# Keys and values of two groups from seven block products, logits in a ring of twelve slots, attend split around the logits

## The chip, the core and the metric

The kernel runs on one core of a Trainium2 chip. The core has five engines that run side by side and wait for each other by semaphores: TensorE (PE in the profile; PEld is its weight load), VectorE (DVE), ScalarE (ACT), GpSimd (POOL) and SyncE (SP), which here only issues DMAs. TensorE writes its results into PSUM, 8 banks of 128 x 512 float32. Everything else lies in SBUF. POOL works on SBUF alone in this kernel.

The metric is the device time of one execution in microseconds, as the median of several runs.

## What is computed

Four cross-attention layers are applied in turn to `x` (4 batches x 512 queries x 256 channels), each against the same context (4 x 1024 tokens x 512 channels). Layers 0, 2 and 3 are "masked": 16 heads of 64, with a bias on a few key columns and an output bias.

```python
def masked_layer(hidden_states, encoder_hidden_states, mask_A, mask_B, Wq, Wk, Wv, Wo, bo, ...):
    q = hidden_states @ Wq;  k = encoder_hidden_states @ Wk;  v = encoder_hidden_states @ Wv
    logits = einsum("bhqd,bhkd->bhqk", heads(q), heads(k)) * 64 ** -0.5 + col_bias
    out = einsum("bhqk,bhkd->bhqd", softmax(logits), heads(v))
    return merge(out) @ Wo + bo + hidden_states
```

Layer 1 is "grouped": an RMS norm of x, 16 query heads of 16 that share 4 key and value heads, no bias, and again the residual.

All matrices are float32. The change touches how `k` and `v` are made, in which order the pieces of attention run, and where their intermediate results lie.

## The kernel before

**Units and steps.** A masked layer of one batch is cut into 8 groups of two heads (128 rows of keys or values), so that 3 layers x 4 batches give 96 masked groups. Layer 1 of one batch is also cut into 8 units, 32 in all. Two lists written by hand, `MASKED_TURNS` and `GROUPED_TURNS` (lines 55 to 62), say for each of 104 steps from which of two streams of batches the next masked group and the next grouped unit come. So 72 steps have a masked group alone, 24 have a masked group and a grouped unit, and 8 have a grouped unit alone. Every instruction is issued in the order of the program; nothing is scheduled afterwards. The order on each engine is therefore what the step loop (from line 963) writes.

**One masked step.** For its group g the step computes the logits, transposed, as 8 tiles of 128 keys x (2 heads x 512 queries): `scores` (line 642). Each tile takes a pair of PSUM banks. ScalarE copies it to SBUF (L662). VectorE takes the running maximum in the first tile's PSUM pair, `mx_place` (L666). `max_quarters` reduces this over the keys (L712, L720, L737), and `max_everywhere` spreads it over all partitions in another PSUM pair, `mb` (L744). VectorE subtracts it from each tile (L749), ScalarE takes the exponentials (L755) and POOL adds the tiles up (L794).

Beside this the step attends for the group of the step before, g1, that is, it multiplies its exponentials with its values (`attend`, L684). It divides by the sums (`normalise`, lines 802 to 830), multiplies finished groups with the output weights (`project_out`, L840), and makes the queries of the next group (L548), the keys of the group after next (L472) and the values of the next group (L514). Keys and values of a group are each one plain product over 512 channels, in four accumulating matmuls of 128 channels. ScalarE copies them out of PSUM (L477, L526).

**Order within a step.** The logits of g come first, then the eight blocks of attend for g1. In a step with a grouped unit `lam`, these alternate with the grouped logits and their exponentials (L616, L639). Then comes a list, `fill`, of projections and products; the list `events`, ordered by rough times, interleaves the subtractions and exponentials of g with it. For a grouped unit that comes next, the maxima of its logits are found by a pass of their own (`maxima_pair`, L616 and L608), also woven into `fill`.

**Space.** The exponentials lie in `st_all`: two rings of 8 tiles and one more for the sum, so that a group has 8 slots of its own and the next group 8 others. A grouped unit uses the slots of the ring that is free. The transposed context of a batch, `ctx`, is one tile [128, 4, 1024], and three such tiles are held. PSUM banks are handed out in program order by the class `Place` (line 95). A width of 2 takes the pair of banks that was given back longest ago, a width of 1 the bank that was given back longest ago, with some preference for one whose neighbour is taken.

**Transfers.** `load_masked` and `load_grouped` issue the weights' DMAs on SP: 256 KB for the keys of one group, 256 KB for its values, 128 KB each for its query and output weights.

## Time and profile before

| What | Value |
|---|---|
| Median of 3 runs | 3808.88 us (3807.39 to 3809.19) |
| Time of the profiled execution | 3809.19 us |
| Its span, first to last instruction | 3807.4 us |
| Granted TensorE clock, mean | 0.997 of full speed |
| Keys: L472, busy on TensorE | 689.6 us in 1,536 instructions |
| Values (masked and grouped): L514 | 742.3 us in 6,400 instructions |
| Logits: L652 | 708.3 us in 3,072 instructions |
| Attend: L684 | 805.7 us in 4,064 instructions |
| DMA, mean over the span | 26 GB/s |

A float32 matmul shows as two MATMUL instructions, so that 1,536 rows of L472 are 768 matmuls of the program. The "busy" time of a group counts overlapping instructions once. The "mean" of one MATMUL is longer than its share of the busy time, because one starts before the last has ended. The idle time in a row is that of the engine just before those instructions, with the one that ended it.

### The profile page before, as it was taken

Reading aid. Unit: us, or ns where it says so; the run is one execution under the profiler, and the core shown is the slowest. Engines: PE = TensorE matmul, PEld = TensorE weight load, DVE = VectorE, ACT = ScalarE, POOL = GpSimd, SP = SyncE. Lnnn points to the kernel's source line nnn. Section 1 sums busy time; section 2 is a strip of 40 time slices with the busy share of each in tenths; the row PEclk is TensorE's granted clock in tenths of the full one; section 3 lists DMA queues with packets and bytes.
Section 4 is the critical chain, followed back from the end, with each engine's and each line's share of the span. In section 5 each row is a group of like instructions: output and inputs, shape, how many; then the busy total and the mean of one; then the engine's idle time right before and its main releaser. Section 6 shows DMA issues by size and latency. Waiting matters only on the chain.

```text
span 3807.4 us, 50450 instructions
## 1 busy us (share of the span) xinstructions
PE 3741.1 (98%) x19662; PEld 1879.9 (49%) x19662; DVE 3001.7 (79%) x3928; ACT 2101.8 (55%) x2433; POOL 1624.5 (43%) x749
## 2 busy tenths in 40 slices
PE   8999999999999999999999999999999999999998
PEld 4555444554434555555545444555444355555554
DVE  6887778778877888888887887788787778888887
ACT  4555455555545555555555555555555455555554
POOL 3555113443313555555553333445332155555554
PEclk9999999999999999999999999999999999999999
DMA  2111000010000001101011010100100000000100
GB/s 67 42 31 26 12 24 18 17 33 22 19 11 23 26 26 42 37 26 31 26 25 36 27 27 18 29 26 19 28 20 23 11 25 26 25 26 26 31 24 7
DMA packets 187874, 98.71 MB, mean 26 GB/s; under 512 B 43240, under 2 KB 183528, under 8 KB 187636
## 3 DMA queue, kind: packets, MB, share of 16 engines
q1 hardware_dynamic: 182510, 82.90, 7.9%
q0 software_dynamic: 2560, 8.39, 0.8%
q10 hardware_dynamic: 2566, 4.20, 0.5%
q8 instruction: 155, 2.54, 0.3%
q14 instruction: 83, 0.68, 0.1%
HBM read 89.16 MB, written 2.10 MB: 24 GB/s over the span
## 4 chain that ended last, share of the span: by engine, by line
PE 87%; DVE 8%; ACT 2%; issue 2%; DMA 0%; POOL 0%; DVEq 0%; ACTq 0%; POOLq 0%
PE ps L514 19%; PE ps L684 19%; PE ps L472 17%; PE ps L652 13%; PE ps L616 7%; PE ps L840 5%; PE ps L548 5%; DVE ps L666 4%; ACT st L662 1%; DVE st L749 1%; DVE st L608 1%; PE ps L490 1%; PE ps L658 1%; DVE qt L634 1%; PE ps L704 0%
## 5 line engine op out<-in xcount | busy, mean ns | idle before, releaser
L794 POOL TENSOR_TENSOR st<-st 128x1024 f32<-128x1024 f32 x668 | 1579.7, 2365 | 2059.7 <-ACT st L755 2015.7
L666 DVE TENSOR_TENSOR ps<-ps,st 128x1024 f32<-128x1024 f32 x672 | 828.2, 1232 | 466.3 <-ACT st L662 407.4
L755 ACT ACTIVATE st<-st 128x1024 f32<-128x1024 f32 x768 | 783.2, 1054 | 707.1 <-DVE st L749 695.2
L749 DVE TENSOR_TENSOR st<-st,ps 128x1024 f32<-128x1024 f32 x768 | 885.0, 1212 | 3.3
L684 PE MATMUL ps<-st,v 128*64 128x512 f32 (+1 forms) x4064 | 805.7, 597 | 0.5 <-DVE st L608 0.5
L662 ACT COPY st<-ps 128x1024 f32<-128x1024 f32 x768 | 715.4, 1047 | 101.8 <-PE ps L658 81.4
L514 PEld LDWEIGHTS ps<-wv,ctx 128*128 128x128 f32 x6400 | 729.8, 192 | 73.9 <-issue 63.6
L514 PE MATMUL ps<-wv,ctx 128*128 128x128 f32 x6400 | 742.3, 276 | 0.6 <-ACT st L662 0.6
L652 PE MATMUL ps<-qt,kt 64*128 64x512 f32 x3072 | 708.3, 598 | 1.4 <-ACT qt L554 1.4
L472 PE MATMUL ps<-ctx,wk 128*128 128x512 f32 x1536 | 689.6, 598 | 2.2 <-ACT ctx L384 2.2
L684 PEld LDWEIGHTS ps<-st,v 128*64 128x64 f32 (+1 forms) x4064 | 233.5, 130 | 545.6 <-issue 480.7
L472 PEld LDWEIGHTS ps<-ctx,wk 128*128 128x128 f32 x1536 | 288.1, 191 | 389.1 <-issue 373.2
L652 PEld LDWEIGHTS ps<-qt,kt 64*128 64x128 f32 x3072 | 283.8, 186 | 326.4 <-ACT st L662 146.0
L526 ACT COPY v<-ps 128x512 f32<-128x512 f32 x200 | 117.1, 585 | 497.1 <-PE ps L514 493.2
L608 DVE TENSOR_TENSOR st<-st,ps 128x1024 f32<-128x1024 f32 x224 | 273.3, 1220 | 129.8 <-PE ps L616 61.2
L616 PE MATMUL ps<-qt,kt 32*128 32x512 f32 x2048 | 323.8, 645 | 28.1 <-DVE qt L634 16.3
L639 ACT ACTIVATE st<-ps 128x1024 f32<-128x1024 f32 x256 | 248.4, 1023 | 185.2 <-PE ps L616 156.7
L840 PE MATMUL ps<-ot,wo 128*128 128x512 f32 x448 | 217.4, 611 | 1.4 <-DVE ot L829 0.7
L616 PEld LDWEIGHTS ps<-qt,kt 32*128 32x128 f32 x2048 | 103.4, 186 | 214.1 <-issue 57.1
L548 PE MATMUL ps<-x,wq 128*128 128x512 f32 x384 | 185.6, 606 | 1.8 <-ACT x L356 1.1
L477 ACT COPY kt<-ps 128x512 f32<-128x512 f32 x192 | 109.8, 572 | 77.3 <-PE ps L472 77.0
L840 PEld LDWEIGHTS ps<-ot,wo 128*128 128x128 f32 x448 | 78.5, 189 | 135.2 <-issue 124.2
(143 smaller groups left out, 1633.2 us busy)
## 6 DMA issues: line engine op xcount, KB each, us to landing
wk<-in_L_xattn_Wk_dram SPq DMA_DIRECT2D x96, 256.0 KB
wv<-in_L_xattn_Wv_dram SPq DMA_DIRECT2D x96, 256.0 KB
wq<-in_L_xattn_Wq_dram SPq DMA_DIRECT2D x96, 128.0 KB
wo<-in_L_xattn_Wo_dram SPq DMA_DIRECT2D x96, 128.0 KB
qt<-qt ACTq DMA_DIRECT2D x32, 128.0 KB
xraw<-in_x_dram SPq DMA_DIRECT2D x3, 512.0 KB
out_dram<-out SPq DMA_DIRECT2D x3, 512.0 KB
wq<-in_L_xattn_wq_dram SPq DMA_DIRECT2D x32, 32.0 KB
```

The source lines that it names most:

```text
L472: nc.tensor.matmul(m, lhsT=g.wk[:, k, :], rhs=ctx_t[g.b][:, k, n * 512 : (n + 1) * 512], start=(k == 0), stop=(k == KT - 1),)
L514: nc.tensor.matmul(m[:, t * P : (t + 1) * P], lhsT=ctx_t[g.b][:, k, (4 * n + t) * P : (4 * n + t + 1) * P], rhs=g.wv[:, k, :], start=(k == ...
L548: nc.tensor.matmul(m, lhsT=g.wq[:, k, :], rhs=x[:, k, :], start=(k == 0), stop=(k == KC - 1))
L616: nc.tensor.matmul(ws[odd].ap[:, j * S : (j + 1) * S], lhsT=g.kt[rows, i * P : (i + 1) * P], rhs=g.qt[rows, :], start=True, stop=True,)
L652: nc.tensor.matmul(m[:, j * S : (j + 1) * S], lhsT=g.kt[g.rows[j], keys], rhs=g.qt[g.rows[j], :], start=True, stop=t > 0,)
L662: nc.scalar.copy(g.st[t], m)
L666: nc.vector.tensor_tensor(top, top, g.st[t], ALU.max)
L684: nc.tensor.matmul(g.po[at, :], lhsT=g.v[:, t, rows], rhs=g.st[t][:, j * S : (j + 1) * S], start=(t == first), stop=(t == last),)
L749: nc.vector.tensor_tensor(g.st[t], g.st[t], g.mb, ALU.subtract)
L755: nc.scalar.activation(st, st, AF.Exp)
L794: nc.gpsimd.tensor_tensor(g.acc, g.st[0] if t == 1 else g.acc, g.st[t], ALU.add)
L840: nc.tensor.matmul(m[:, k * S : (k + 1) * S], lhsT=g.wo[:, k * P : (k + 1) * P], rhs=g.ot, start=True, stop=True,)
```

## The change

The whole change is made of these parts.

- **Seven products for eight.** The weights of two neighbouring groups form a 2 x 2 arrangement of blocks (two halves of the 512 channels by two groups), and so does the context (two halves of the channels by two halves of the tokens). A scheme of Strassen's kind in Winograd's form makes the four result blocks from seven block products and a number of sums. `pair_products` computes keys or values of a pair of groups so. In odd-numbered groups' steps the keys of the next pair are made, in even-numbered groups' steps the values of the pair itself.
- **Sums on POOL.** The sums of weight blocks (`combine_weights`, four of 128 x 256 for each pair and kind), of products (seven of 128 x 512 for each pair and kind) and of context blocks (four of 128 x 1024 for each batch) are `tensor_tensor` on GpSimd. ScalarE copies each product out of PSUM first.
- **Contexts.** A batch's context becomes a tile [128, 14, 512] that holds four blocks and three sums of blocks; two such tiles are held instead of three. One block, S3, is stored with A11 taken away, so that the grouped layer, which needs the block itself, adds A11's product again: its keys and values take more matmuls.
- **Ring.** `st_all` becomes 15 slots: a ring of 12 for exponentials, two for sums, one for the grouped maximum. The logits of group n use slots 8n to 8n + 7 modulo 12, so that its last four tiles lie where the first four of the group before were. A grouped unit uses four slots in turn.
- **Attend split.** Blocks 0 to 3 of attend for g1 come before the logits of g, blocks 4 to 7 after them. The grouped attend is spread between the grouped exponentials. Query and output projections move to the front of `fill`, or, in steps with a grouped unit, between its exponentials.
- **Maximum and sums.** The reduction over keys goes through PSUM with one more copy, the spread maximum lies in the first tile's own pair (`mx_place`) until the last subtraction, and the subtractions and exponentials have new times. The running sums from the third tile on are issued at the start of the next step. `normalise` of a group comes one step later, as VectorE's first work in a step.
- **Weights.** One DMA of 512 KB brings the weights of a pair.
- **Turns.** 106 steps: 74 with a masked group alone, 22 with both, 10 with a grouped unit alone.

The instructions that change in number, as the two programs are built (matmuls of the program, not MATMUL rows):

| Engine | Instruction | Before | After |
|---|---|---|---|
| PE | masked keys, 512 columns | 768 | 674 |
| PE | values, 128 columns (masked and grouped) | 3200 | 2848 |
| PE | grouped keys | 64 of 512 columns | 160 of 256 columns |
| POOL | sums of 128 x 1024 | 668 | 682 |
| POOL | sums of 128 x 512 | 0 | 665 |
| POOL | sums of 128 x 256 | 0 | 380 |
| ACT | copies of 128 x 512 out of PSUM, keys and values | 392 | 677 |
| DVE | small copies and sums of the reductions over keys | 1291 | 1561 |

The core of the diff:

```diff
     class Place:
-        def __init__(self, width=2):
+        def __init__(self, width=2, beside=None):
...
                 at = min(free, key=lambda n: free[n] + (2 if n ^ 1 in free else 0))
+                if beside and beside.banks[0] ^ 1 in free:
+                    at = beside.banks[0] ^ 1
...
-    st_all = t_([P, 2, NT + 1, 2 * S], "st", "st")
+    st_all = t_([P, 15, 2 * S], "st", "st")
+    ACC, TOP = 12, 14
...
+    def ring(n):
+        return st_slot(n % 12)
...
+    def combine_context(b):
+        x = lambda i: of_context(b, i)
+        on_pool(x(S1), x(S3), x(A22), ALU.add)
+        on_pool(x(S2), x(S1), x(A11), ALU.subtract)
+        on_pool(x(S4), x(A12), x(S2), ALU.subtract)
...
+    def combine_weights(kind, q):
+        w = weights[kind, q]
+        t = t_([P, 3, 2, P], "t2", f"t{kind}_{masked[2 * q].name}")
...
+        on_pool(t3, b12, b22, ALU.subtract)
+        on_pool(b12, b12, b11, ALU.subtract)
+        on_pool(t2, b22, b12, ALU.subtract)
+        on_pool(t4, b21, t2, ALU.subtract)
...
+    def pair_products(kind, q):
...
+        def product(i, w, out_, then):
+
+            place = Place(1)
+            m = place.ap
+            x = of_context(b, i)
+            if kind == "k":
+                for k in range(2):
+                    nc.tensor.matmul(m, lhsT=w[:, k, :], rhs=x[:, k, :], start=k == 0, stop=k == 1)
...
+            def done():
+                nc.scalar.copy(out_, m)
+                place.back()
+                then()
...
+        def p2():
+            return product(A12, b21, to(0, 0), lambda: add(to(0, 0), u2))
...
+        return [(1.75, p) for p in (p1, p2, p6, p7, p4, p5, p3)]
...
     def scores(g, within):
-        g.st = [st_slot((NT + 1) * g.ring + t) for t in range(NT)]
-        g.mx = st_slot((NT + 1) * g.ring + NT)
+        g.st = [ring(NT * g.n + t) for t in range(NT)]
+        g.mx = st_slot(ACC + g.n % 2)
...
+    def over_keys(of, op):
+
+
+        w = Place(1)
+        quarter, half = w.ap[:, 0:32], w.ap[0:64, 32:64]
+        other = t_([64, 32], "other", f"other{len(turns)}")
+        turns.append(0)
+        over_quarter(quarter, of, op)
+        nc.vector.tensor_copy(other, quarter[64:128, :])
+        nc.vector.tensor_tensor(half, quarter[0:64, :], other, op)
+        nc.vector.tensor_copy(other[0:32, :], half[32:64, :])
+        return half[0:32, :], other[0:32, :], w
...
+    def max_everywhere(g):
+
+        one, other, w = over_keys(g.mx_place.ap, ALU.max)
+        every = t_([P, 2 * S // 32, 1], "every", f"every_{g.name}")
         for h in range(4):
...
+            nc.vector.tensor_tensor(every[32 * h : 32 * (h + 1), :, 0], one, other, ALU.max)
+        w.back()
+        g.mb = g.mx_place.ap
...
+        for w in summed[:4]:
+            w()
+        if kind:
+            combine_weights(kind, q)
+        for w in summed[4:]:
+            w()
+        summed.clear()
+        if attended_last:
+            normalise(attended_last)
+            outs = [attended_last] + outs
+        attended_last = g1
...
+        if g1 and (g or lam):
+            place_out(g1)
         if g:
...
+            if g1:
+                attend(g1, range(0, 4))
             scores(g, lambda: lower_queries(lam) if lam else None)
...
+            max_everywhere(g)
         if lam:
...
+            if g:
+                for t in range(4):
+                    subtract(g, t)
             for i in range(NT // 2):
                 if g1:
-                    attend(g1, range(2 * i, 2 * i + 2))
+                    blocks = range(4, 8) if g else range(NT)
+                    attend(g1, blocks[2 * i : 2 * i + 2])
                 if coming and not g:
                     pair(i)
                 exponentials_pair(lam, i)
...
+                if i:
+                    if fill and (i > 1 or g):
+                        run([fill.pop(0)])
+                    if i == 1:
+                        place_out(lam, 1, g1.place if g1 else None)
+                    attend(lam, range(2 * i - 2, 2 * i))
...
         elif g1 and g:
-            attend(g1)
...
+            attend(g1, range(4, 8))
...
+        if kind:
+            made = pair_products(kind, q)
+            if len(fill) > 1 and not lam and not coming:
+
+                made[-1:-1] = [fill.pop()]
+            fill += made
```

## The prediction

> **What bounds the kernel now.** I read the page first: busy shares, then the chain, then the costliest groups.
>
> ```profile
> PE 3741.1 (98%) x19662; PEld 1879.9 (49%) x19662; DVE 3001.7 (79%) x3928; ACT 2101.8 (55%) x2433; POOL 1624.5 (43%) x749
> ...
> L794 POOL TENSOR_TENSOR st<-st 128x1024 f32<-128x1024 f32 x668 | 1579.7, 2365 | 2059.7 <-ACT st L755 2015.7
> L666 DVE TENSOR_TENSOR ps<-ps,st 128x1024 f32<-128x1024 f32 x672 | 828.2, 1232 | 466.3 <-ACT st L662 407.4
> ...
> L514 PE MATMUL ps<-wv,ctx 128*128 128x128 f32 x6400 | 742.3, 276 | 0.6 <-ACT st L662 0.6
> ...
> L472 PE MATMUL ps<-ctx,wk 128*128 128x512 f32 x1536 | 689.6, 598 | 2.2 <-ACT ctx L384 2.2
> ```
>
> TensorE carries 87% of the chain; keys (L472) and values (L514) are 1,432 us of it, and the change attacks these. The starts of the mask matmuls (L658) in the timeline give the length of each step: 31.94 us for a plain masked step (32.82 with a piece of context transposed), about 49 us (mean 47.8) where a grouped unit runs beside it, some 24 us for a grouped unit alone. A plain step in the timeline, from 1508.84 to 1541.66 (columns: start, length, engine, instruction, count):
>
> ```profile
> 1508.84 1.13 PE L652 MATMUL ps<-qt,kt 64*128 64x512 f32 x4
> ...
> 1509.81 0.38 PE L658 MATMUL ps<-aug_q,aug_k 64*128 64x512 bf16 x2
> ...
> 1510.28 7.43 ACT L662 COPY st<-ps 128x1024 f32<-128x1024 f32 x8 [0.75 <-PE ps L658]
> ...
> 1512.24 9.26 DVE L666 TENSOR_TENSOR ps<-ps,st 128x1024 f32<-128x1024 f32 x7 [5.00 <-ACT st L662]
> ...
> 1516.12 7.09 PE L684 MATMUL ps<-st,v 128*64 128x512 f32 x32
> ...
> 1521.53 1.25 DVE L712 TRANSPOSE_TENSOR_REDUCE quarter<-ps 128x32 f32<-128x1024 f32 x1
> ...
> 1523.04 0.83 DVE L737 TENSOR_TENSOR every<-half 32x32 f32<-32x32 f32 x4
> 1523.14 1.99 PE L840 MATMUL ps<-ot,wo 128*128 128x512 f32 x4
> ...
> 1526.68 7.03 PE L472 MATMUL ps<-ctx,wk 128*128 128x512 f32 x16
> ```
>
> See that TensorE has no gap: logits 7.28 us (1508.84 to 1516.12), attend 7.02, output 1.82, queries 1.72, keys 6.9, values 7.2 make the step. VectorE's maximum runs from 3.40 to 12.66 us after the first logit matmul, and its `every` (L737) ends 15.0 us after it, all hidden: the keys' and values' matmuls have other PSUM banks to go to. A matmul instruction of 512 columns starts every 0.43 us (weight loads of L472), one of 128 columns every 0.113 (7.22 us for 64).
>
> **Products.** Per pair of groups, 14 instead of 16 double matmuls of 512 columns for keys, the same share for values. Each step now makes keys or values of one pair: 28 x 0.43 = 12.04 us, or 112 x 0.113 = 12.65, where it made 6.9 + 7.2 = 14.1. That is 1.75 us a step; over 94 and 96 pairs' halves about 165 us, if TensorE stays the bound.
>
> **POOL.** Added per step: 4 weight sums of 128x256 and 7 sums of 128x512. No such row exists; L794's 1024 elements take 2.43 us from start to start, and POOL's memsets scale with elements (0.53 at 512, 0.31 at 256), so I take 1.25 and 0.67. Lower end: exactly half and a quarter; upper end: 2.43 each, as if length did not matter. POOL's step is then 7 x 2.43 + 7 x 1.25 + 4 x 0.67 = 28.4 us, inside a step of 32 to 33, though in order. Weight sums stand behind four running sums: they begin about 13 us into the step; the 512 KB they wait for are issued at its start, and the timeline's 1 us windows show 512 KB issued from 1533.7 on moved by 1537.2. Hidden. The running sums of t=2 and 3, which now must precede the copies of logits 6 and 7 into the same ring slots, end about 8 us into the step, those copies start after 10. Hidden by 2 us. SP issues fewer transfers (one of 512 KB for two of 256); the queue has nothing late.
>
> The skill speaks against loading POOL: "SBUF — State Buffer", section "Who interferes with whom", says a VectorE instruction with two SBUF inputs shuts out, or waits for, a GpSimd instruction that reads SBUF. The row first: L799 (both inputs in SBUF) takes 692 ns, L829 (one in PSUM) 691, so here no such wait shows; but POOL mostly rests at L799. The change moves the small sums of VectorE to one PSUM input; left are 24 such instructions (L799, L595). By the rule at most 24 x 2.43 = 58 us, by the row 0. I take 0: their results are not due within the step.
>
> **Logits, two PSUM pairs for three.** The changed program's bank addresses show that 91 of its 96 logits passes rotate over two pairs, where before all had three: `place_out` for the attended group now comes before the logits. Tile t+2 must wait for the copy of tile t. From the rows: first copy starts 1.44 us after the first matmul, each lasts 1.05, back to back every 0.93; a restarted tile takes 1.13 to its end, and ScalarE follows 0.09 later. Tile 3 then starts at 3.42 instead of 2.90, and two tiles take 1.13 + 0.1 + 1.05 = 2.28 instead of 1.72; the pass lasts 8.95, 1.67 more. "TensorEngine Tiling (Array Packing)", section "PSUM Bottleneck", warns that tiled matmuls outrun the copy out of PSUM. As a rate that would cost 7.43 - 7.28 = 0.15 us; the rows say it is latency and 1.67. I take the rows.
>
> **The bank behind the maximum.** In all but a handful of the steps without a grouped unit (66) the first product's bank is the one `over_keys` of the same group's maximum has just used. So it waits for `every`. After: attend of four blocks 3.59 (half of 7.02, and a switch 0.08), first copied tile 3.40, seven maxima 9.26, reduction 1.28, three small instructions 0.65 (a third one is new), `every` 0.83: 19.0 us. TensorE would be there at 3.59 + 8.95 + 3.59 + 1.82 = 17.95. It idles 1.1 us, and this hides the logits' wait. Step: 19.06 + 12.04 (or 12.65) + 1.72 = 32.8 or 33.4, mean 33.1, **+1.16 x 66 = +77 us**. Behind it on VectorE stand the output's addition and eight subtractions, to 31; `normalise` (4.2) then ends 2 us into the next step, before its maximum is due at 7. ScalarE's exponentials and copies reach 2 us into the next step, its first copy is due at 5. Both covers hold by 2 to 5 us.
>
> **Steps with a grouped unit (22).** TensorE's own work falls to about 46 (-1.8). But VectorE now does `normalise` between the last maxima of the grouped unit (the last pair closes the step) and the new maximum: 2.6 + 2.7 + 1.2 (mean) + 4.2, so the maximum begins about 10.7 instead of 7.0 us into the step. `lower_queries`' result stands behind its fifth instruction, so the first grouped exponentials wait for about 18 us, TensorE being there at 15. Then each pass needs four banks while the maximum holds two and the two `po` share a pair: query and output projections wait for a bank about 1 us each. By hand 54 to 55 us for a step of 49, +5.5; the floor is -1.8. Half the attends, which filled these waits, have gone ahead of the logits. I take +3.5, nearer the hand count: **+77 us**.
>
> **Rest.** Grouped keys: 28 us become 160 half-width matmuls; with two columns' halves beside each other 34, one after the other 69. The new order has several of the same half in a row, so +25. Grouped values 32 x 0.22 = +7. Two steps fewer shared, two more plain and two more alone: 2 x (32.1 + 23.8 - 47.8) = +16. The first step makes one pair instead of four halves, with one more key half ahead: -9.
>
> **Sum:** 77 + 77 + 25 + 7 + 16 - 9 = +193 on the profiled run's 3809.2 (span 3807.4; the median, 3808.9, is the same): **4000 us, 5% slower.**
>
> **Rivals.**
> - *VectorE's bank is no bound* (0.20): the maximum runs earlier than I have it, steps are TensorE's own sum of 32.0, grouped ones as before: 3809 + 4 + 25 + 7 + 16 - 9 = 3852.
> - *Faster* (0.13): TensorE's saving stays whole, neither bank nor pair stalls it. Speaks for it: 98% busy before and no gap. Against: the bank addresses. Plain step 30.3, -1.64 x 66 = -108; shared steps at their floor, -40; rest with grouped keys at +6, +20: 3681. It decides from the point where the first product's bank is free by 16.3 us of the step.
> - *POOL is the bound* (0.10): 512 elements cost 1.6 us, 256 cost 0.85; 31.6 us of work with waits between, steps of 34.5, about 4100.
> - The change not doing what it says is excluded: the built program has 282 + 376 + 16 key and 2,688 masked value matmuls for 768 and 3,072.
>
> **The numbers.** The main case has 0.50, its own range 3900 to 4080. Between the cases near 3809 lie 0.07. A measurement of this kernel tells 0.2%, 8 us: faster 0.13, same 0.04, slower 0.83. The range leaves out the faster side and the far end of POOL's: 3820 to 4105.
>
> **What would show it.** Plain steps of 33 between mask matmuls, the first product's matmul waiting for `every` about 1 us; weight loads of the logits waiting for copies of L662's successor 0.5 to 0.6 us at tiles 3, 5 and 7; POOL near 2,690 us busy; shared steps above 51. Plain steps at 30.3, or a first product without a wait, would make the forecast wrong.

## The result and the profile after

The changed kernel takes 4229.56 us (median of 4 runs, 4229.32 to 4229.77) against 3808.98 us before: **1.1105 times as long**, 95% interval 1.1086 to 1.1124. The forecast was 4000 us with a range to 4105: the direction was right, the size was not, 193 us forecast and 420 measured.

The page of the changed kernel (span 4227.6 us; after the bar: busy us, mean ns of one | idle before, and its releaser) has these lines for those shown of before:

```profile
PE 3868.6 (92%) x18962; PEld 1776.6 (42%) x18962; DVE 3078.5 (73%) x4198; ACT 2259.2 (53%) x2718; POOL 2761.9 (65%) x1808
...
L905 POOL TENSOR_TENSOR st<-st 128x1024 f32<-128x1024 f32 x666 | 1574.4, 2364 | 614.3 <-ACT st L871 583.9
L778 DVE TENSOR_TENSOR ps<-ps,st 128x1024 f32<-128x1024 f32 x672 | 828.2, 1232 | 495.3 <-ACT st L774 440.4
...
L764 PE MATMUL ps<-qt,kt 64*128 64x512 f32 x3072 | 844.8, 650 | 122.8 <-DVE ot L933 56.0
...
L539 PE MATMUL ps<-wv,ctx 128*128 128x128 f32 x3072 | 373.8, 278 | 29.1 <-DVE every L857 29.1
...
L534 PE MATMUL ps<-ctx,wk 128*128 128x512 f32 x752 | 361.6, 615 | 37.9 <-DVE every L857 37.8
```

Of before, the prediction shows keys and values; the logits' row is

```profile
L652 PE MATMUL ps<-qt,kt 64*128 64x512 f32 x3072 | 708.3, 598 | 1.4 <-ACT qt L554 1.4
```

TensorE fell from 98% to 92% busy, and waits now stand at three groups that had next to none. One logit matmul (L764) takes 650 ns where it took 598: part of the busy time is a slower clock or waiting inside a group. TensorE's waits, sorted (us in total, times, longest us):

```profile
PE ps L764 <- DVE ot L933: 56.0, 16, 6.0
PE ps L534 <- DVE every L857: 37.8, 33, 3.7
PE ps L764 <- ACT st L774: 37.1, 150, 0.5
PE ps L539 <- DVE every L857: 29.4, 33, 1.2
PE ps L944 <- ACT st L751: 22.1, 22, 1.3
PE ps L764 <- DVE short L918: 20.2, 5, 4.3
```

`every` is the wait the forecast named. `ot` and `short` it did not have: they belong to `normalise` of the group before.

Where the time went is read from the starts of the mask matmuls (L658 before, L770 after) in the timeline, one per masked step. The differences, grouped by kind of step (mean us, count in brackets; the last rows are sums of us), for before, after, and four of the experiments below:

| kind of step | before | after | e3_bank | h2_end_bank | h3_always | r1_out_of_loop |
|---|---|---|---|---|---|---|
| plain | 31.99 (58) | 33.61 (59) | 32.44 | 32.41 | 32.41 | 32.43 |
| shared with a grouped unit | 47.71 (22) | 56.38 (20) | 56.40 | 52.80 | 52.81 | 51.12 |
| last before a grouped run (first logits) | 47.95 (3) | 53.36 (3) | 53.05 | 53.49 | 48.46 | 47.99 |
| the one before that (grouped keys) | 42.89 (4) | 46.58 (4) | 45.41 | 45.42 | 45.41 | 45.41 |
| first behind a grouped run | 32.80 (4) | 35.88 (4) | 35.56 | 35.58 | 34.33 | 34.32 |
| a step and the units alone behind it, sum | 336.2 (3) | 510.9 (4) | 517.0 | 515.4 | 505.4 | 482.1 |
| whole span | 3807.4 | 4227.6 | 4157.8 | 4084.1 | 4053.3 | 3996.2 |

Before's very last step, 26.1 us, is among its plain ones. So the 420 us are: plain steps 59 x 1.62 = 96; shared steps 20 x 8.67 = **173**; the three kinds at the ends of grouped runs 16 + 15 + 12 = 43; stretches with units alone, like for like, 73 (a step and four units 133.5 to 159.3, a shared step and two 101.3 to 122.5 and 123.4, an opening step and two 101.6, put together from before's parts, to 105.6); the new turns at before's own prices 38 (one plain step and one stretch of 101.6 more, two shared steps fewer); first step -9; the two ends 6.

### The profile page after: what moved, and what is told of

Same layout as the page of the kernel before. It is cut to its first block, busy times and chain, and to the rows that moved or that the text cites. A ratio compares the mean times of both kernels' runs of the same rounds, so it can differ in the third digit from the quotient of the medians.

```text
span 4227.6 us, 50531 instructions
## 1 busy us (share of the span) xinstructions
PE 3868.6 (92%) x18962; PEld 1776.6 (42%) x18962; DVE 3078.5 (73%) x4198; ACT 2259.2 (53%) x2718; POOL 2761.9 (65%) x1808
## 4 chain that ended last, share of the span: by engine, by line
PE 55%; DVE 28%; ACT 11%; issue 3%; POOL 2%; DMA 0%; DVEq 0%; ACTq 0%; POOLq 0%
DVE ps L778 15%; PE ps L539 12%; PE ps L534 11%; PE ps L796 10%; PE ps L728 6%; PE ps L764 5%; PE ps L660 5%; ACT st L871 4%; DVE ps L824 4%; ACT st L774 3%; DVE st L720 3%; PE ps L944 2%; DVE every L857 1%; PE ps L603 1%; PE ps L626 1%
## 5 line engine op out<-in xcount | busy, mean ns | idle before, releaser
L764 PE MATMUL ps<-qt,kt 64*128 64x512 f32 x3072 | 844.8, 650 | 122.8 <-DVE ot L933 56.0
L796 PE MATMUL ps<-st,v 128*64 128x512 f32 (+1 forms) x4064 | 847.4, 603 | 17.9 <-ACT qt L666 11.7
L764 PEld LDWEIGHTS ps<-qt,kt 64*128 64x128 f32 x3072 | 271.6, 194 | 651.3 <-ACT st L774 331.5
L720 DVE TENSOR_TENSOR st<-st,ps 128x1024 f32<-128x1024 f32 x224 | 273.5, 1221 | 311.4 <-ACT st L718 177.0
L796 PEld LDWEIGHTS ps<-st,v 128*64 128x64 f32 (+1 forms) x4064 | 225.9, 130 | 573.9 <-issue 464.5
L728 PE MATMUL ps<-qt,kt 32*128 32x512 f32 x2048 | 385.4, 660 | 69.0 <-DVE st L720 15.8
L539 PE MATMUL ps<-wv,ctx 128*128 128x128 f32 x3072 | 373.8, 278 | 29.1 <-DVE every L857 29.1
L539 PEld LDWEIGHTS ps<-wv,ctx 128*128 128x128 f32 x3072 | 358.3, 192 | 98.4 <-DVE every L857 55.6
L534 PE MATMUL ps<-ctx,wk 128*128 128x512 f32 x752 | 361.6, 615 | 37.9 <-DVE every L857 37.8
L349 POOL TENSOR_TENSOR v<-v,u_v 128x512 f32<-128x512 f32 x192 | 244.5, 1275 | 177.5 <-ACT v L544 171.0
L349 POOL TENSOR_TENSOR kt<-kt,u_k 128x512 f32<-128x512 f32 x188 | 239.3, 1275 | 158.2 <-ACT kt L544 151.7
L539 PE MATMUL ps<-tv,ctx 128*128 128x128 f32 x2304 | 267.3, 275 | 0.8 <-DVE x L966 0.4
L539 PEld LDWEIGHTS ps<-tv,ctx 128*128 128x128 f32 x2304 | 261.7, 192 | 6.4 <-POOL u_v L349 4.5
L534 PE MATMUL ps<-ctx,tk 128*128 128x512 f32 x564 | 252.6, 594 | 0.0
```

The source lines that it names most:

```text
L349: nc.gpsimd.tensor_tensor(out_, one, other, op)
L534: nc.tensor.matmul(m, lhsT=w[:, k, :], rhs=x[:, k, :], start=k == 0, stop=k == 1)
L539: nc.tensor.matmul(m[:, cols], lhsT=x[:, k, cols], rhs=w[:, k, :], start=k == 0, stop=k == 1)
L720: nc.vector.tensor_tensor(g.mx, g.mx, w.ap, ALU.max)
L728: nc.tensor.matmul(ws[odd].ap[:, j * S : (j + 1) * S], lhsT=g.kt[rows, i * P : (i + 1) * P], rhs=g.qt[rows, :], start=True, stop=True,)
L764: nc.tensor.matmul(m[:, j * S : (j + 1) * S], lhsT=g.kt[g.rows[j], keys], rhs=g.qt[g.rows[j], :], start=True, stop=t > 0,)
```

## What the trace after shows of a plain and of a shared step

A plain step in the timeline of the changed kernel, from its first logits to its first product (start, length, engine, line, operation, count, idle before it):

```profile
1612.51 1.13 PE L764 MATMUL ps<-qt,kt 64*128 64x512 f32 x4
...
1621.47 3.65 PE L796 MATMUL ps<-st,v 128*64 128x512 f32 x16
...
1625.15 1.26 DVE L824 TRANSPOSE_TENSOR_REDUCE ps<-ps 128x32 f32<-128x1024 f32 x1
...
1627.12 0.77 DVE L857 TENSOR_TENSOR every<-ps,other 32x32 f32<-32x32 f32 x4
...
1627.94 3.70 PE L534 MATMUL ps<-ctx,wk 128*128 128x512 f32 x8 [0.90 <-DVE every L857]
```

The logits' pass lasts 8.96 us (1612.51 to 1621.47), for 8.95 forecast and 7.28 before. The product then has the wait of the forecast, 0.90 us for 1.1, and undisturbed plain steps are 32.94 and 33.43 us in turn, for 32.8 and 33.4 forecast.

The start of a shared step (mask matmul at 2412.95) in the same view:

```profile
2412.35 0.72 DVE L682 STREAM_TRANSPOSE st<-ps 128x512 f32<-128x512 f32 x1
...
2413.37 1.01 ACT L774 COPY st<-ps 128x1024 f32<-128x1024 f32 x1 [6.76 <-DVE short L683]
...
2414.13 1.54 DVE L910 TENSOR_TENSOR ot<-o,ot 128x512 f32<-128x512 f32 x1
2415.60 1.25 DVE L824 TRANSPOSE_TENSOR_REDUCE ps<-st 128x32 f32<-128x1024 f32 x1
...
2417.55 0.70 DVE L918 TENSOR_TENSOR short<-ps,other 32x16 f32<-32x16 f32 x4
...
2418.30 7.22 PE L764 MATMUL ps<-qt,kt 64*128 64x512 f32 x18 [4.06 <-DVE short L918]
...
2419.32 0.69 DVE L933 TENSOR_TENSOR ot<-ps,ot 128x512 f32<-128x512 f32 x1
...
2420.06 0.50 PEld L764 LDWEIGHTS ps<-qt,kt 64*128 64x128 f32 x2 [1.25 <-DVE ot L933]
...
2420.41 1.01 ACT L774 COPY st<-ps 128x1024 f32<-128x1024 f32 x1 [6.03 <-PE ps L764]
```

VectorE still has the grouped normalisation (L682 to L910) when the step begins. The second logit tile needs the bank in which `normalise` reduces its sums (released at `short`), the third the bank of the output that it scales (released at `ot`). As the program hands banks out in this step, the reduction has bank 5 and the output bank 1; the second tile gets banks 4 and 5, the third 0 and 1. So TensorE stands 4.06 us in the middle of the second tile. The third tile's weight load waits 1.25 us more, this time behind matmuls that are still running, and the next copy comes after 6.03 us without one. The two waits are not in every shared step: L764 waits for `short` in 5 of the 20 (20.2 us) and for `ot` in 8 (29.2 us). Then the clock: in the table of stretches (columns: stretch, length, busy us of PE, PEld, DVE, ACT and POOL, granted clock, DMA share, GB/s) a stretch of a plain step's length, from the middle of one to the middle of the next, and this shared step read

```profile
3797.50:3830.90 33.40, 31.98 (x125) 13.40 (x125) 27.23 (x37) 19.66 (x24) 28.10 (x18) 1.00 0.07 24
2412.90:2473.50 60.60, 52.75 (x236) 17.72 (x234) 42.24 (x54) 28.98 (x34) 27.12 (x19) 0.94 0.01 2
```

VectorE is busy 42 of 61 us and POOL 27 of 61: neither is full. TensorE waits, and has a lower granted clock besides: 0.50 from 2415.9 to 2422.5, from within the idle of 4.06 us on.

## Experiments

Theory A was that VectorE's order and PSUM banks make the kernel slow; the rivals were POOL's new sums and the seven products themselves.

**e1_eight**: eight plain products in the changed order.

```diff
-        return [(1.75, p) for p in (p1, p2, p6, p7, p4, p5, p3)]
+        return [(3.5, lambda j=j, h=h: product(j, h)) for j, h in ((0, 0), (1, 0), (0, 1), (1, 1))]
```

> The changed kernel with the seven products undone: each step makes the same pair's keys or values by four plain products of 512 contracted channels, and no sum of weights, contexts or products is left on POOL; order of the steps, ring, PSUM places and the split attend stay. Theory A (VectorE's order and the PSUM banks made the changed kernel slow; the products save what they should): the products' 12.04 or 12.65 us go back to 14.1, so 94 steps get 1.75 us longer, about 165 us: 4395 us, plain steps 34.9 between mask matmuls. Theory B (POOL's sums or the seven products themselves made it slow): 4050 us or less, shared steps back near 48. Theory C (the new order of the shared steps, but with POOL's sums in VectorE's way there): plain steps 34.9, shared steps 3 us or more shorter than in the changed kernel, 4250 to 4330.

Measured: 4344.14 us, 115 more than the change. Undisturbed plain steps are 34.71 and 35.27, that is +1.77 and +1.84: the seven products save just what the sum said. But shared steps are 56.85 for 56.38: there the saving is lost, so TensorE's own work alone does not set their length. The step with grouped keys is 45.67 against 46.58 although its products cost 1.77 more: A11's product, which the grouped keys need a second time because of how S3 is stored, costs 2.7 us a step. That they are made in halves costs nothing that shows (in the timeline 7.18 us here, 7.09 before, 9.88 in the changed kernel).

**e2_nosums**: no sums of weights and products on POOL; the keys and values are then not the right ones, and the sums of context blocks stay.

```diff
         def add(one, other):
-            on_pool(one, one, other, ALU.add)
+            pass
```

> The changed kernel without any sum of weights and of products on POOL (left out: the combinations of weights and of products, so keys and values are not the right ones; all matmuls, copies and the context sums stay). Theory A: POOL's sums lie beside other work, the time moves by 0 to -40 us (VectorE's instructions with two SBUF inputs get shorter): 4190 to 4235. Theory B: without them 100 us or more are gone: 4130 or less, shared steps near 50.

Measured: 4238.86 us, 9 more, shared steps 56.31. The sums of weights and products are hidden, and with e1_eight, which has neither them nor the seven products and is slower still, theory B falls.

The context sums are not hidden everywhere. In three plain steps four of them, 9.54 us from 1680.09 on in one, stand on POOL ahead of the running sums, whose slots the last two logit copies need. The copy waits, the maximum is late, and TensorE idles (changed kernel, timeline):

```profile
1691.97 1.01 ACT L774 COPY st<-ps 128x1024 f32<-128x1024 f32 x1 [2.62 <-POOL st L905]
...
1699.52 5.12 PE L534 MATMUL ps<-ctx,wk 128*128 128x512 f32 x8 [3.49 <-DVE every L857]
```

These three steps take 37.0 to 37.5 us, 3 to 5 us more than their like; in e1_eight, which has no context sums, two of the three take what their neighbours take.

**e3_bank**: the first product takes any bank but the reduction's.

```diff
-            place = Place(1)
+            place = Place(1, avoid=last_over[0] if w is b11 else None)
```

> The changed kernel with another PSUM bank for the first product: never the one that the reduction of the maximum has just used; nothing else. Theory A: TensorE stood 1.1 us per plain step at that bank, 66 steps, so -73 us: 4157, plain steps 32.0. If instead the logits' two pairs or a projection's bank hold it up in the same place: 4215 to 4235, plain steps still 33.

Measured: 4156.23 us, -73; plain steps 31.77 and 32.27. Shared steps stay at 56.40. The plain steps' part is settled, and they come out at before's 31.94, not at the 30.3 of TensorE's own work: the two pairs of logits take the rest, as the forecast had it (the pass of 8.96 us above; no run gives the third pair back).

**e4_late**: `normalise` behind the new maximum in shared steps, and the output banks of the two attended groups in one pair.

```diff
         if attended_last:
-            normalise(attended_last)
+            if not (g and lam):
+                normalise(attended_last)
...
-            place_out(g1)
+            place_out(g1, 1, before_last.place if before_last and g and lam else None)
...
             max_everywhere(g)
+        if g and lam and before_last:
+            normalise(before_last)
```

> The changed kernel with one step of VectorE's order changed: where a grouped unit runs beside a masked one, the normalisation of the group before comes behind the new maximum instead of ahead of it, and the two attended groups' PSUM banks share a pair. Theory A (the maximum, late by the normalisation's 4.2 us, holds TensorE up in the shared steps, and idles of over 3 us halve its clock afterwards): shared steps from 56 to 51 or 52, 22 x -4.5 = -100 us, 4130. If VectorE's grouped work at the end of the step before is what makes it late: -20 us or less.

Measured: 4423.04 us, **194 more**; shared steps 64.42. A miss. Its waits name the reason:

```profile
PE ps L796 <- DVE mcol L847: 66.1, 13, 5.5
PE ps L728 <- DVE short L918: 48.4, 19, 3.2
```

The attends now take the bank of the grouped maximum's reduction, and the grouped logits the bank of the later `normalise`. So this run doesn't test the order alone: each move hands out other banks.

**g1_sbuf, g2_po, g3_early, g4_late**: no PSUM bank for the small results of the reductions. g2_po adds e4_late's shared pair, g3_early and g4_late add one more move each to g2_po. (A cut; the two copies between the sums go too, and the banks are no longer given back.)

```diff
     def over_keys(of, op):
-        w = Place(1)
-        quarter, half = w.ap[:, 0:32], w.ap[0:64, 32:64]
+        quarter = t_([P, 32], "quarter", f"quarter{len(turns)}")
+        half = t_([64, 32], "other", f"other{len(turns)}")
```

> The changed kernel with the small results of its reductions over the keys (normalisation, both maxima) in SBUF, so that no reduction holds a PSUM bank; nothing else. Theory A2 (what makes it slow are PSUM banks that VectorE's chain of reductions holds, in plain steps one and in shared steps several; the run before showed that VectorE's order alone isn't it): plain steps as with the other first bank, 31.8 or 32.3 us, -73 us; shared steps lose the waits for the reductions (short, mcol, every), from 56 to 53 or 54: 4080 to 4110 us. Rival (shared steps are held by the time at which VectorE's maximum ends, banks or not): shared steps stay at 56, 4156 us.

> As g1_sbuf, and in shared steps the attended group's bank shares the pair of the group before, so that no logits pair waits for its normalisation. Theory A2: the 16 waits of 3.5 us for ot (56 us) go, and the half clock behind them: shared steps 50 to 52, another -50 to -80 us on g1_sbuf. Rival: TensorE only waits later, for the lowered queries or the maximum: within 15 us of g1_sbuf.

> As g2_po, and the grouped queries are lowered after the third tile of the logits instead of the sixth, so that VectorE does it three maxima (3.8 us) earlier. Theory A2: the first grouped logits then wait no longer for the queries: -20 to -60 us on g2_po, shared steps 49 to 51. Rival (that wait is not the last one): within 10 us of g2_po.

> As g2_po, but the normalisation of the group before behind the new maximum. With e4_late this move cost 194 us. If the banks of its reductions were the reason (Theory A2), it costs nothing here: within 40 us of g2_po, either way. If the order itself is the reason, about 190 us slower than g2_po.

Measured: 4432.61, 4381.27, 4406.37 and 4473.46 us. g1_sbuf is 203 slower than the change, with banks free. VectorE's rows say why; in the changed kernel, where these instructions have at most one SBUF input (the last two have two):

```profile
L918 DVE TENSOR_TENSOR short<-ps,other 32x16 f32<-32x16 f32 x380 | 62.7, 165 | 7.1
L837 DVE TENSOR_TENSOR ps<-ps,other 64x32 f32<-64x32 f32 x223 | 42.7, 191 | 7.6
L910 DVE TENSOR_TENSOR ot<-o,ot 128x512 f32<-128x512 f32 x16 | 18.7, 1170 | 0.6
L707 DVE SCALAR_TENSOR_TENSOR xn<-x,colL_xattn_norm_w,inv 128x512 f32<-128x512 f32 x8 | 18.4, 2340 | 0.4
```

in g1_sbuf, where both inputs lie in SBUF:

```profile
L911 DVE TENSOR_TENSOR short<-other 32x16 f32<-32x16 f32 x380 | 332.1, 874 | 13.0
L833 DVE TENSOR_TENSOR other<-quarter 64x32 f32<-64x32 f32 x223 | 175.3, 786 | 7.7
```

and before the change, where both lay in SBUF too:

```profile
L720 DVE TENSOR_TENSOR half<-quarter 64x32 f32<-64x32 f32 x128 | 24.0, 187 | 4.4
```

Whether POOL runs beside them decides it. In g1_sbuf 172 of L833's 223 sums overlap a POOL instruction in time and take 964 ns on average; the other 51 take 187. In the changed kernel, with one input in PSUM, L837 takes 191 ns either way. Before, none of L720's 128 rows overlaps a POOL instruction, nor any of the 16 of L799, from whose 692 ns the prediction read that no wait shows. L910 in the shared step above, 1.54 us long, lies wholly beside POOL's running sums (2407.92 to 2417.88 in the timeline). This agrees with the rule of the Trainium skill's "SBUF — State Buffer", section "Who interferes with whom", which the prediction weighed and set to 0. As remedies these four are void: g2_po and g3_early differ from g1_sbuf by -51 and -26 us, with waits of up to 11 us for `mcol`, `ot` and `st` still there. g4_late against g2_po (+92) settles nothing about order.

**h2_end_bank**: e3_bank, and `normalise` at the end of the step in which the group was attended, where a grouped unit follows.

```diff
         if attended_last:
-            normalise(attended_last)
+            if not at_end:
+                normalise(attended_last)
             outs = [attended_last] + outs
         attended_last = g1
+        at_end = bool(g1 and coming and (g or lam))
...
+        if at_end:
+            late.append(lambda: normalise(g1))
```

> As e3_bank, and wherever a grouped unit follows, a group is normalised at the end of the step in which it was attended (as before the change), behind its subtractions and ahead of the grouped maxima, where VectorE idles 6.4 us, and not at the start of the next step. Theory A3 (banks held at the start of the shared steps by the normalisation: the second and third tile of the logits lie in its reduction's and in its output's bank): the waits of L764 for short and ot (76 us) go, VectorE's maximum begins 4 us earlier, no half clock behind: shared steps 50 to 52, -100 to -140 us on e3_bank: 4020 to 4055. Rival (the normalisation's place doesn't matter, or costs at the new place what it saved): 4140 or more.

Measured: 4083.11 us, -73 on e3_bank: less than expected, but the mechanism holds. Shared steps are 52.80. The start of the step shown above in the timeline of this run (mask matmul at 2332.65):

```profile
2332.87 1.88 PE L764 MATMUL ps<-qt,kt 64*128 64x512 f32 x8
2335.05 2.04 PE L764 MATMUL ps<-qt,kt 64*128 64x512 f32 x8 [0.30 <-ACT st L774]
```

The wait of 4.06 us is gone, and 0.30 us for a copy is left. In all shared steps the 49 us of waits for `short` and `ot` are gone, and the steps are 72 us shorter. The move takes both the banks and VectorE's work away from the start of the step, and no run separates the two. That it is the bank is read from the trace: the matmul that waits reads nothing of `normalise`; it writes into bank 5, where `normalise` had its sums.

**h3_always**: the same in every step.

```diff
-        at_end = bool(g1 and coming and (g or lam))
+        at_end = bool(g1 and (g or lam))
```

> As h2_end_bank, but every group is normalised at the end of the step in which it was attended. In plain steps VectorE's order stays what it was (the end of one step borders on the start of the next). Theory A3: the eight waits of L764 for ot that h2_end_bank still has (30 us, up to 6.0 each, in the steps in which grouped units begin) go, and the half clock behind them: -30 to -45 us, 4038 to 4053; first grouped steps from 53.5 to 49 us. Rival (VectorE's own lateness at these places, from the root-mean-square norm's instructions, is what holds it up, whichever bank): within 10 us of h2_end_bank.

Measured: 4053.07 us, -30. The last steps before grouped runs go from 53.49 to 48.46, before's 47.95. What TensorE still waits for in the shared steps lies at the projections between the grouped passes: L947 (the output's) waits for a bank that an exponential frees, L796 (an attend) behind the copy of the projected queries:

```profile
PE ps L947 <- ACT st L751: 21.7, 22, 1.4
...
PE ps L796 <- ACT qt L666: 11.7, 17, 0.7
```

**r1_out_of_loop**: h3_always, with these projections behind the passes.

```diff
-                    if fill and (i > 1 or g):
+                    if fill and i > 1 and not g:
                         run([fill.pop(0)])
...
-            if fill:
+            if fill and not g:
                 run([fill.pop(0)])
```

> As h3_always, with the query and output projections of the shared steps behind the four passes of grouped logits and not between them (where they were before the change). Theory (in the passes each projection waits 0.7 to 1.2 us for a bank that an exponential frees, and this is most of what the shared steps have too much): shared steps from 52.8 to 50 or less, -50 us or more, 4000. Rival (without the projections TensorE waits in the passes for the exponentials, 1.94 us a pass, instead): within 15 us of h3_always, shared steps above 52.

Measured: 3992.16 us, -61, ratio to before 1.0480 (1.0463 to 1.0498): the best version found, and still slower than before. Shared steps fall less than expected, to 51.12 (-34 us in all); the stretches with units alone give -23.

**r2_spread**: r1_out_of_loop with filling matmuls, and the last attended blocks one per pass. Two of these four blocks are then multiplied by grouped exponentials, which by that time hold their slots of the ring, so part of the context product is left out.

```diff
-                    attend(g1, blocks[2 * i : 2 * i + 2])
+                    attend(g1, blocks[i : i + 1] if g else blocks[2 * i : 2 * i + 2])
```

> r1_out_of_loop and k3_fill6 together, and the last four attended blocks one per pass instead of two in the first two passes. If the passes wait for exponentials, work spread over them hides it: 5 to 30 us below the better of the two. If not, the same as their sum.

Measured: 4043.19 us. It tells nothing of spreading, since the late blocks had to wait for the exponentials; it does show that the ring of 12 slots fixes these attends to the first two passes.

**k1_warm, k2_fill, k3_fill6**: does TensorE's lower clock come from its idles?

```diff
+            if g and lam:
+                idle = Place(1)
+                for i in range(12):
+                    nc.tensor.matmul(
+                        idle.ap[0:64, :], lhsT=ones[:, 0:64], rhs=ctx_t[coming.b][:, i % 4, :],
+                        start=True, stop=True,
+                    )
+                idle.back()
             lower_queries(coming)
```

(k2_fill; k3_fill6 has 6 for 12 and h3_always under it; k1_warm adds zeros behind the second tile of the logits.)

> The changed kernel with 16 matmuls more in each shared step, between the second and the third tile of the logits: zeros times exponentials, added to the attended group's sums (they add nothing), 3.5 us of TensorE's work where it waits 3 to 6 us. Theory (idles of over 3 us halve TensorE's clock for some 3 us afterwards): the clock stays up, 20 to 60 us less than the changed kernel, granted clock above 0.98 in these steps. Rival (the lower clock costs nothing, since VectorE sets the pace): 0, or up to 22 x 3.5 = 77 us more.

> As h2_end_bank, with 12 matmuls more (5.3 us, ones times context into a free bank, used by nobody) at the two places where TensorE idles 5.4 us for mcol ahead of two grouped units alone. Theory (an idle of that length halves the clock for about 3 us): the 32 matmuls of L741 behind it take 1.08 us and not 1.94, the 8 of L796 1.94 and not 3.58, and the two stretches of 126.8 and 125.1 us get 2 to 3 us shorter each. Rival (those matmuls are slow for another reason, the release of a bank for one): they stay at 1.94 and 3.58.

> As h3_always, with the idle-filling matmuls of k2_fill cut from 24 instructions, which took 10.5 us, to 12, which should take 5.3, the length of the idle. Theory (the half clock behind that idle costs time on the path): the two stretches of 126.6 us get 2.5 to 5 us shorter each, their granted clock from 0.89 to 0.95, -5 to -10 us in all. Rival (other waits swallow it): no shorter than 126.

k1_warm: 4327.83 us, +98. A bad test: the instruction that waits is the second half of the second tile, so the zeros stood behind the wait, and they took 7.1 us and more, not 3.5. k2_fill settles the question for these two places. In h2_end_bank, in the timeline, and then the stretch around it in the table of stretches:

```profile
2100.01 1.94 PE L741 MATMUL ps<-ident,mcol 128*32 128x128 f32 x32 [5.37 <-DVE mcol L850]
2101.88 3.58 PE L796 MATMUL ps<-st,v 128*64 128x512 f32 x8
```

```profile
2044.50:2171.30 126.80, 109.73 (x528) 35.55 (x526) 73.99 (x105) 50.41 (x58) 29.80 (x19) 0.89 0.04 8
```

and in k2_fill, where the idle is filled:

```profile
2095.88 10.52 PE L1253 MATMUL ps<-ctx,ones 128*64 128x512 f32 x24
2106.32 1.08 PE L741 MATMUL ps<-ident,mcol 128*32 128x128 f32 x32
2107.34 1.94 PE L796 MATMUL ps<-st,v 128*64 128x512 f32 x8
```

```profile
2044.00:2171.00 127.00, 114.62 (x554) 37.13 (x548) 73.98 (x105) 50.50 (x58) 31.54 (x21) 0.95 0.03 7
```

Behind the idle both groups run at half speed, without it at full speed, and the granted clock goes from 0.89 to 0.95. The filling took 10.5 us for an idle of 5.4, so the total stays (4086.63 us). At the right length, k3_fill6: 4044.12 us, -9 on h3_always, the two stretches 126.6 to 125.9 and 126.7 to 119.6: the sum as expected, but unevenly spread over the two. The granted clock differs in the same way: it goes from 0.89 to 0.91 in the first, to 0.96 in the second. The runs' ranges overlap (4039.0 to 4046.03 against 4043.77 to 4055.04). That the clock costs time on the path is likely, not sure.

**s1_eight_mended**: r1_out_of_loop with the eight products of e1_eight. **s2_early**: r1_out_of_loop with the queries lowered after the fourth tile.

```diff
-            if t == 5:
+            if t == 3:
                 within()
```

> r1_out_of_loop with eight plain products for seven, as in e1_eight. Theory (in the changed kernel's shared steps TensorE waited for VectorE and for banks, so that the products' saving was lost there: e1_eight's shared steps were only 0.5 us longer; in r1_out_of_loop TensorE is the bound again): now every one of the 94 steps that make products gets 1.75 us longer, shared ones too, +150 to +170 us on r1_out_of_loop, 4140 to 4160. Rival (the shared steps are still bound by something else): shared steps within 0.7 us of 51.1, +115 us, 4107.

> r1_out_of_loop with the grouped queries lowered after the fourth tile of the logits, not the sixth. Theory (six waits of L728 for qt, 16.8 us, are left because VectorE lowers the queries behind five maxima): -10 to -25 us. Rival (TensorE waits for the maximum or the logits' copies instead): within 8 us, or slower.

s1_eight_mended: 4129.94 us, +138, between the two expectations. Plain steps get 1.67 longer, shared ones 0.46 (51.58 for 51.12): more work on TensorE still hardly lengthens the shared steps, although TensorE is busy 49.0 of 51.1 us there in r1_out_of_loop (47.0 of 47.7 before). s2_early: 3992.79 us, no difference.

## Why the prediction was right in direction and wrong in size

The forecast is 227 us short. Of these, 96 stand in the shared steps, 73 in the stretches of units alone, 31 in the plain steps (with those behind grouped runs), 22 in the turns; the rest are small terms of both signs. Two steps of the argument failed: the price of the shared steps, and the missing price of the units alone.

- **Products**, -1.75 us a step: right. e1_eight shows 1.77 to 1.84 in plain steps. In shared steps they are worth 0.5.
- **POOL hidden**: right for what it priced. A sum of 128x512 takes 1275 ns for 1.25 us forecast; without the sums nothing is gained (e2_nosums). It left out the context sums, which cost some 4 us in each of three steps.
- **Bank behind the maximum, logits over two pairs**, +1.16 us in 66 steps, 77: right in mechanism and size. The waits are 37.8 + 29.4 us, 1.02 each, the pass of the logits is 8.96 us for 8.95, the undisturbed steps are 32.94 and 33.43, and e3_bank takes 73 us away.
- **Steps with a grouped unit**, +3.5 us each: **the first step that failed**. Measured +8.67. The forecast saw that `normalise` now stands ahead of the maximum, but charged it only as lateness of VectorE. It didn't look up whose banks the second and third logit tiles get: those of `normalise` itself. So TensorE stands at the start of the step, before any maximum is due: 49 us in all, and at half clock behind it. h2_end_bank takes 3.6 us of the 8.67 away by moving the `normalise`, r1_out_of_loop another 1.7 with the projections' waits, which the forecast had named, at about 1 us each. The hand count said 5.5, and I took 3.5 "nearer the hand count"; nothing in the profile paid for that discount. Of the other 3.4 us, 1.4 are more idle time of TensorE than before (2.1 us a step for 0.7) and 2.1 are more busy time, in part at half clock. What is behind them is open; the lowered queries aren't it (s2_early).
- **Clock**: missing in the forecast, although the trace of before has a small case of it. An idle of 2.06 us stands ahead of grouped logits, and behind it the granted clock is 0.50 for 6.8 us (timeline, then table of stretches):

```profile
517.87 7.80 PE L616 MATMUL ps<-qt,kt 32*128 32x512 f32 x32 [2.06 <-DVE qt L634]
```

```profile
519.00:525.80 6.80, 6.80 (x28) 2.90 (x24) 4.82 (x9) 6.29 (x7) 0.00 (x0) 0.50 0.01 2
```

An idle of 2.07 us at 3033.7 leaves the clock at 1.00. In the changed kernel every idle of TensorE of 2.7 us or more goes with a stretch at half clock, and those of about 1 us in plain steps leave it at 1.00. "TensorE: Matmul & The Clock Gate", Part 1 of the Trainium skill, has the clock halved after an idle window of about 3.4 us; the idles of 4.06 and 5.37 us agree, the one of 2.06 us is shorter than that, so the page's figure is no safe limit here. k2_fill shows that the idle is the cause. The half clock lasts 24 us in all before and 230 after. TensorE is busy for 176 of these 230, so an estimate from the trace is that at most 88 us were lost to it; how much of that lies on the path was not measured, except that the two idles of k3_fill6 were worth some 9 us. The forecast had a wait of about 3 us by hand and should have asked this.
- **Two SBUF inputs**, 0 taken, at most 58: 16 x (1170 - 692) + 8 x (2340 - 748) ns = 20 us of VectorE's time; L910 is part of what stands ahead of `normalise` in the shared step shown. The rule was right and the row misleading: POOL did not only "mostly" rest at L799, it rested at all 16.
- **Grouped keys +25, values +7**: the keys' step is +3.7 with the bank's 1.2 in it; A11's second product costs 2.7 x 4 = 11. Too dear in the forecast.
- **Turns +16**: 38. The new turns begin a grouped run once more than before, which the forecast didn't count.
- **Units alone**: **the second step that failed**. The forecast put them at nothing, without a reason; measured +73. The fill of the step before now ends too early (TensorE idles 5.4 us for `mcol`, then runs at half clock), and r1_out_of_loop returns 23 of it. The rest is open.
- **Rivals**: POOL as the bound (4100) is nearest to the measured time but wrong in its mechanism. The two with lower times fall by the 66 waits for `every`.

So the seven products are worth 115 to 138 us here. The order that makes room for them (two context tiles, a ring of 12, attends ahead of the logits, new turns) costs over 500: e1_eight has it without the products, at 535 us over before. Of the loss, 237 us could be had back (4229.56 to 3992.16); without the products that order still stands 321 us over before (s1_eight_mended). Its parts were not varied one by one, nor were the turns, 38 us.

## What to carry to other kernels

When a step moves on one engine, list the PSUM banks it holds and who takes them next; a wait moves with the bank, not with the instruction. Price a hand-counted stall at its full length, and look in the trace for what the clock does behind stalls of that length: here it was at half for 6.8 us from within an idle of 4.06 us on. A row that shows no contention proves it only for the load that the other engine had beside that row; look whether the two overlap in time at all.

## What was not expected of the hardware

A VectorE sum of 64x32 with both inputs in SBUF takes 187 ns when no POOL instruction runs beside it and 964 on average when one does; moving 1,115 such small instructions to SBUF cost 203 us on balance, although it freed the banks. And filling an idle of 5.4 us with work that nobody uses made the matmuls behind it twice as fast (1.94 to 1.08 us for 32, 3.58 to 1.94 us for 8).
